# Expert slots without a token gather a row of their own number instead of row 0

## The chip, the core and the metric

The kernel runs on one core of a Trainium2 chip. The metric is the device time of one execution in microseconds; the figure for a kernel is the median of its runs. The profile is one further execution, recorded by the hardware profiler. Clock values are the granted TensorE clock as a share of full speed.

## What is computed

The reference is two transformer layers on 2048 tokens of width 128, all in float32. Layer 0 is attention with 16 heads and then a mixture of 16 experts; layer 1 is causal attention with 8 heads and then a token-shift block. What matters here is the expert part of layer 0, cut to its core:

```python
logits = hidden @ router_w.T                      # 2048 x 16
top_vals, top_idx = top_k(logits, 1)              # one expert a token
scores = sigmoid(logits at top_idx, -inf elsewhere)
routed_in = hidden[None] * scores.T[:, :, None]
gate, up = split(einsum('nth,nhf->ntf', routed_in, gate_up_proj), 2)
routed_out = einsum('ntf,nfh->nth', up * silu(gate), down_proj)
out = shared_ffn(hidden) + routed_out.sum(axis=0)
```

The router's choice for the reference's inputs gives the experts 0 to 15 these numbers of tokens: 101, 145, 126, 158, 178, 94, 189, 85, 135, 99, 88, 198, 96, 132, 123, 101.

## The kernel before

**Slots.** The kernel sorts tokens by expert. It has `SLOTS = 31` slots of 128 rows, which is what 2048 tokens on 16 experts need at worst. Each expert takes as many whole slots as it needs, in the order of the experts. For the counts above that is 23 slots (0 to 22); slots 23 to 30 hold no token, and the last slot of an expert is partly filled (slot 2 holds 17 tokens, slot 13 holds 7, slot 20 holds 4). 31 x 128 = 3968 rows stand for 2048 tokens, so 1920 rows are spare.

**From place to row number.** Lines 850 to 872 work out on DVE the place `slot` of each token, its slot's start `hi` and its row in the slot `lo`. Line 877 compares `hi` with the starts of all slots (`in_tile`, 1 where token and slot belong together), line 881 multiplies this by the token's number (`in_tile_r`), line 887 compares `lo` with 0 to 127 (`at`), and line 890 multiplies the two on PE: 16 matmuls, one per 128 tokens, add up in PSUM tile `tok_ps` (128 x 32). Each entry is the number of the token that stands at this row of this slot. Nothing adds to a spare entry: it stays 0. Line 893 turns the table into whole numbers, `tok`.

**Gather and experts.** Line 912 issues 31 indirect DMAs from POOL, one per slot: each reads 128 rows of 512 bytes from the DRAM tensor `hs_rows` (the scaled tokens, written at line 782) at the numbers in one column of `tok`, into `xs`. Slots go through PE in quads of four: `gathered` (line 926) turns the four tiles (transposes L921, copied out of PSUM by ACT L923) and loads the number of each slot's expert into a PE register (L929); `up_gate` (L935) multiplies by the expert's weights, `silu_up` works on ACT and DVE (L804 to L806), `turn_act` transposes the result (L921, ACT copy L923), `down` (L948) multiplies again, and DVE L952 and an SP DMA (L953) send the rows to `y_rows`. The loop (line 956) takes quads 0 to 7 in order, with `up_gate(q)`, `down(q - 2)`, `gathered(q + 1)`, a step of the shared FFN (L826, L814) at even q, and `turn_act(q - 1)`. At the end 16 more indirect DMAs (L970) fetch each token's row from `y_rows` into `yx`, which DVE adds to `x` (L987). Rows of spare entries are computed and written to `y_rows` too, and never fetched.

**Order.** Each engine works in the order that the framework's scheduler gave its instructions; an instruction that waits holds back what stands behind it on the same engine. The indirect DMAs have POOL's queue to themselves in this stage; the `y_rows` writes have SP's.

Of the kernel before, what the change touches and what calls it, by code (L numbers as in the profile page):

```python
# [9 lines left out]
F32 = mybir.dt.float32  # L10
F32R = mybir.dt.float32r
# [3 lines left out]
ALU = mybir.AluOpType  # L15
# [3 lines left out]
P = 128  # L19
T = 2048  # L20
NT = T // P
# [21 lines left out]
def two_layers(ctx: ExitStack, tc: tile.TileContext, a: dict, out: bass.AP):  # L43
    nc = tc.nc
# [104 lines left out]
    token = const.tile([P, NT], F32, name="token")  # L149
# [594 lines left out]

    hT = h1[:, HOFF:]

    a1 = ctx.enter_context(ExitStack())
# [6 lines left out]
    with ExitStack() as s:  # L756
        rp = s.enter_context(tc.tile_pool(name="route", bufs=1))
# [6 lines left out]
        pt = s.enter_context(tc.tile_pool(name="moet", bufs=2, space=PSUM))  # L764
# [8 lines left out]
        for b in range(NB):  # L773
            ps = pt.tile([P, QB], F32, name=f"hs_ps{b}", tag="t")
            for i in range(TB):
                t = b * TB + i
                nc.tensor.transpose(ps[:, i * P:(i + 1) * P], hT[:, t * P:(t + 1) * P], ident)
            for i in range(TB):
                t = b * TB + i
# [6 lines left out]
        ps = po.tile([P, QB], F32, name="gb_ps", tag="y")  # L786
# [58 lines left out]
        for t in range(NT):  # L845
            nc.tensor.matmul(pos[:, t + 1:, :], ones_r,
                             mine[:, t:t + 1, :].to_broadcast([P, NT - t, NE]),
                             start=False, stop=(t == NT - 1), skip_group_check=True)
# [20 lines left out]
        hi = rp.tile([P, NT], F32, name="hi")  # L869
# [3 lines left out]


        NSL = SLOTS + 1
        in_tile = rp.tile([P, NT, NSL], F32, name="in_tile")
        nc.vector.tensor_tensor(in_tile, hi.unsqueeze(2).to_broadcast([P, NT, NSL]),
                                iota[:, :NSL].unsqueeze(1).to_broadcast([P, NT, NSL]),
                                ALU.is_equal)
        in_tile_r = rp.tile([P, NT, NSL], F32R, name="in_tile_r")  # L880
        nc.vector.tensor_tensor(in_tile_r, in_tile,
                                token.unsqueeze(2).to_broadcast([P, NT, NSL]), ALU.mult)
        at = rp.tile([P, NT, P], F32R, name="at")
        ps = pt.tile([P, NSL], F32, name="tok_ps", tag="t")
        for b in range(NB):
            cols = slice(b * TB, (b + 1) * TB)
            nc.vector.tensor_tensor(at[:, cols, :], lo[:, cols].unsqueeze(2).to_broadcast([P, TB, P]),
                                    units.unsqueeze(1).to_broadcast([P, TB, P]), ALU.is_equal)
        for t in range(NT):
            nc.tensor.matmul(ps, at[:, t, :], in_tile_r[:, t, :], start=(t == 0),  # L890
                             stop=(t == NT - 1))
        tok = rp.tile([P, NSL], U32, name="tok")
        nc.vector.tensor_copy(tok, ps)

        passed = rp.tile([1, SLOTS, NE], F32, name="passed")
        nc.vector.tensor_tensor(passed, iota[:1, :SLOTS].unsqueeze(2).to_broadcast([1, SLOTS, NE]),
# [135 lines left out]
    with ExitStack() as s:  # L1032
        rp = s.enter_context(tc.tile_pool(name="mixc", bufs=1))
# [4 lines left out]
        for b in range(NB):  # L1038
# [3 lines left out]
            for i in range(2):  # L1042
                t = wp.tile([P, QB], F32, name=f"mt{b}{i}", tag=f"mt{i}")
# [16 lines left out]
            t = wp.tile([P, QB], F32, name=f"ft{b}", tag="ft")  # L1060
# [69 lines left out]
```

## Time and profile before

| what | value |
|---|---|
| median of 3 runs | 1290.14 us (1289.53, 1290.14, 1297.87) |
| the profiled execution's own time | 1296.39 us |
| its span, first to last instruction | 1294.7 us |
| mean granted clock | 0.933 |
| PE busy | 1166.7 us, 90% |
| DVE busy | 958.2 us, 74% |
| ACT busy | 776.4 us, 60% |
| POOL busy | 112.3 us, 9% |
| `xs` gathers (L912) | 31 issues, 849.4 to 887.1 us |
| `yx` gathers (L970) | 16 issues, 936.8 to 955.5 us |

The span falls into attention of layer 0 (to about 815 us), the expert stage (about 815 to 960 us), attention of layer 1 and the last block. Start times in the views count from the span's start. In a timeline row the bracket at the end is the idle time of the engine before this row and what ended it; "issue" is time in which the profile shows nothing that the engine waited for, "remote" a semaphore update whose sender the profile could not name. Ends of matmuls are modelled.

### The profile page before, as it was taken

The page shows a single profiled execution, that of the slowest core. Times are in us where ns is not written, and L with a number is a line of the kernel's source. Part 1 is how long each engine was busy: PE and PEld are TensorE (multiplying, and loading weights), DVE is VectorE, ACT ScalarE, POOL GpSimd, SP SyncE. Part 2 cuts the span into 40 slices and gives each one's busy share as a digit, 9 for nine tenths or more (in the row PEclk, how much of TensorE's full clock was granted, in tenths as well). Part 3 has the DMA queues.
Part 4 walks back from the last instruction along what each step waited for, and adds up shares of the span by engine and source line. Part 5 has one row for each costly group of instructions (what it writes and reads, how often), then busy time and mean ns, then how long its engine had stood idle before and what let it go on. Part 6 is the DMA issues. An engine that isn't in the chain of part 4 may idle for free.

```text
span 1294.7 us, 22355 instructions
## 1 busy us (share of the span) xinstructions
PE 1166.7 (90%) x9243; PEld 528.8 (41%) x9243; DVE 958.2 (74%) x1494; ACT 776.4 (60%) x857; POOL 112.3 (9%) x173
## 2 busy tenths in 40 slices
PE   5579999999999999999999999854977999999986
PEld 3233443444334344334434434533643444444432
DVE  4788888989888898898898841531468779897225
ACT  6117777777777777777777787401312355656763
POOL 2010000000000000000000000253041111100113
PEclk9659999999999999999999999876976799999998
DMA  4831000000000010000000000413211001000001
GB/s 127 112 37 34 3 2 2 2 19 18 1 2 2 3 34 2 2 2 2 2 2 1 2 2 1 131 38 34 57 31 33 19 15 29 7 1 1 2 1 32
DMA packets 25317, 27.38 MB, mean 21 GB/s; under 512 B 5328, under 2 KB 18896, under 8 KB 24704
## 3 DMA queue, kind: packets, MB, share of 16 engines
q1 hardware_dynamic: 21440, 20.50, 7.4%
q0 software_dynamic: 1504, 3.08, 1.6%
q10 hardware_dynamic: 2272, 2.36, 0.8%
q8 instruction: 73, 1.20, 0.4%
q14 instruction: 28, 0.23, 0.1%
HBM read 9.88 MB, written 4.13 MB: 11 GB/s over the span
## 4 chain that ended last, share of the span: by engine, by line
PE 77%; DVE 11%; ACT 4%; issue 3%; another core or an unknown queue 2%; DMA 1%; POOL 1%; POOLq 0%; ACTq 0%; DVEq 0%; SPq 0%
PE a0bank L468 23%; PE a0p L442 17%; PE a0p L377 12%; PE a1bank L468 5%; PE a1p L442 4%; DVE a0mx L381 3%; PE a1p L377 2%; DVE a1mx L381 2%; PE a1p L448 2%; DVE a1masked L386 2%; PE sg L826 2%; ACT a0e L452 1%; PE gu L935 1%; PE a0bank L499 1%
## 5 line engine op out<-in xcount | busy, mean ns | idle before, releaser
L381 DVE TENSOR_REDUCE a0mx<-a0p 128x2 f32<-128x1024 f32 x512 | 623.6, 1224 | 78.0 <-PE a0p L377 68.4
L452 ACT ACTIVATE a0e<-a0p 128x1024 f32<-128x1024 f32 x512 | 521.7, 1024 | 172.5 <-PE a0p L442 147.2
L468 PE MATMUL a0bank<-a0e,vA 128*32 128x256 f32 x4096 | 333.6, 392 | 0.6 <-ACT a0e L452 0.6
L377 PE MATMUL a0p<-kS,a0qS 64*128 64x512 f32 x1024 | 248.2, 481 | 26.4 <-DVE a0mx L381 13.4
L442 PE MATMUL a0p<-a0qS,kS 64*128 64x512 f32 x1024 | 259.8, 497 | 0.0
L452 ACT ACTIVATE a1e<-a1p 128x1024 f32<-128x1024 f32 (+3 forms) x160 | 143.1, 896 | 97.4 <-PE a1p L448 94.4
L442 PEld LDWEIGHTS a0p<-a0qS,kS 64*128 64x128 f32 x1024 | 97.1, 184 | 204.3 <-issue 128.8
L377 PEld LDWEIGHTS a0p<-kS,a0qS 64*128 64x128 f32 x1024 | 100.3, 192 | 111.3 <-ACT a0e L452 58.1
L468 PEld LDWEIGHTS a0bank<-a0e,vA 128*32 128x32 f32 x4096 | 86.4, 108 | 139.2 <-issue 124.9
L381 DVE TENSOR_REDUCE a1mx<-a1p 128x2 f32<-128x1024 f32 x96 | 115.6, 1222 | 20.8 <-PE a1p L377 19.9
L468 PE MATMUL a1bank<-a1e,vA 128*32 128x256 f32 (+1 forms) x1152 | 97.5, 385 | 0.5 <-POOL a1e L455 0.4
L442 PE MATMUL a1p<-a1qS,kS 64*128 64x512 f32 (+3 forms) x320 | 76.4, 472 | 3.1 <-DVE a1mx L381 1.9
L377 PE MATMUL a1p<-kS,a1qS 64*128 64x512 f32 (+3 forms) x320 | 68.3, 429 | 7.1 <-DVE a1mx L386 4.1
L386 DVE CUSTOM_DVE_ANT_0 a1masked<-a1p,later 128x128 f32<-128x128 f32 (+3 forms) x128 | 62.5, 489 | 13.3 <-PE a1p L377 8.5
L977 POOL MEMSET vA<- 128x16 f32 x1 | 0.1, 128 | 718.4 <-PE a0bank L520 718.4
L448 PE MATMUL a1p<-a1mT,a1ones 64*128 64x512 f32 (+3 forms) x320 | 61.8, 378 | 0.0
L442 PEld LDWEIGHTS a1p<-a1qS,kS 64*128 64x128 f32 x320 | 31.1, 190 | 60.9 <-issue 33.4
L377 PEld LDWEIGHTS a1p<-kS,a1qS 64*128 64x128 f32 x320 | 32.7, 199 | 36.1 <-DVE a1mx L386 10.3
L455 POOL TENSOR_SCALAR_AFFINE_SELECT a1e<-a1e 128x256 f32<-128x256 f32 x64 | 26.0, 406 | 233.7 <-ACT a1e L452 233.7
L468 PEld LDWEIGHTS a1bank<-a1e,vA 128*32 128x32 f32 x1152 | 25.4, 108 | 43.0 <-issue 32.8
L935 PE MATMUL gu<-wgu_sb,xsT 128*128 x62 | 18.5, 451 | 20.0 <-issue 19.5
L411 ACT CAST a0mT<-a0bank 8x512 fp32r<-8x512 f32 x16 | 9.2, 574 | 45.4 <-PE a0bank L410 45.3
(330 smaller groups left out, 795.7 us busy)
## 6 DMA issues: line engine op xcount, KB each, us to landing
kS<-a0qS SPq DMA_DIRECT2D x28, 128.0 KB
wgu_sb<-in_gate_up SPq DMA_DIRECT2D x1, 2048.0 KB
a0qS<-a0qh SPq DMA_DIRECT2D x62, 32.0 KB
a0qS<-a0ql SPq DMA_DIRECT2D x62, 32.0 KB
y_rows<-y SPq DMA_DIRECT2D x7, 256.0 KB
a1qS<-a1qh SPq DMA_DIRECT2D x24, 64.0 KB
a1qS<-a1ql SPq DMA_DIRECT2D x24, 64.0 KB
hs_rows<-hs SPq DMA_DIRECT2D x4, 256.0 KB
```

The source lines that it names most:

```text
L377: nc.tensor.matmul(ps[:, j, :n], qS[b][r:r + RT, st, i * P:(i + 1) * P], kS(st)[r:r + RT, kb * QB:kb * QB + n], start=True, stop=True)
L381: nc.vector.tensor_reduce(pm[:, i, 2 * pair:2 * pair + 2, kb], ps, AX.X, ALU.max)
L386: nc.vector.tensor_tensor_reduce(masked[:, :n], ps[:, j, :n], later[:, QB - n:], 1.0, LOWEST, ALU.add, ALU.max, pm[:, i, g, kb:kb + 1])
L411: nc.scalar.copy(mT, ps[:nm_rows])
L442: nc.tensor.matmul(ps[:, j, q0:], kS(st)[r:r + RT, kt * P:(kt + 1) * P], qS[b][r:r + RT, st, q0:], start=True, stop=fused)
L448: nc.tensor.matmul(ps[:, j, q0:], ones[r:r + RT, g // S, :], shift[u][r:r + RT, q0:], start=False, stop=True)
L452: nc.scalar.activation(e[:, :, q0:], ps[:, :, q0:], AF.Exp, scale=scale)
L455: nc.gpsimd.affine_select(out=e[:, :, q0:q0 + P], in_=e[:, :, q0:q0 + P], compare_op=ALU.is_ge, fill=0.0, base=0, pattern=[[0, 2], [1, P]] ...
L468: nc.tensor.matmul(av[g * W:(g + 1) * W, c0:c1], vA(kt, grp * HG + g), held[kt, g // 2][:, g % 2, c0:c1], start=(kt == 0 and c0 == 0), sto ...
L499: nc.tensor.transpose(ps[:, i * P:(i + 1) * P], o[:, i * P:(i + 1) * P], ident)
L826: nc.tensor.matmul(ps[:, j, :], w[:, k * P:(k + 1) * P], hT[:, b * QB:(b + 1) * QB], start=True, stop=True)
L935: nc.tensor.matmul(ps[:, i, :], xsT[q][:, i * P:(i + 1) * P], wgu[:, bass.ds(regs[j], 1), :].rearrange("p a f -> p (a f)"), start=True, st ...
```

## The change

The table of row numbers gets a second half. `in_tile` now holds both factors side by side, the comparison (index 1) and its product with the token number (index 0), so one matmul of 64 columns instead of 32 gives the token number and the count of tokens (1 or 0) for each entry. DVE then computes `spare` = (count - 1) x token and subtracts it from the number. For a filled entry `spare` is 0. For a spare entry in row p of slot j the result is `token[p, j mod 16]` = 128 x (j mod 16) + p instead of 0. So the 128 entries of an unused slot read 128 different, adjacent rows of `hs_rows`. The number of DMAs and the bytes that they move stay as they are.

```diff
         NSL = SLOTS + 1
-        in_tile = rp.tile([P, NT, NSL], F32, name="in_tile")
-        nc.vector.tensor_tensor(in_tile, hi.unsqueeze(2).to_broadcast([P, NT, NSL]),
+        in_tile = rp.tile([P, NT, 2, NSL], F32R, name="in_tile")
+        nc.vector.tensor_tensor(in_tile[:, :, 1, :], hi.unsqueeze(2).to_broadcast([P, NT, NSL]),
                                 iota[:, :NSL].unsqueeze(1).to_broadcast([P, NT, NSL]),
                                 ALU.is_equal)
-        in_tile_r = rp.tile([P, NT, NSL], F32R, name="in_tile_r")
-        nc.vector.tensor_tensor(in_tile_r, in_tile,
+        nc.vector.tensor_tensor(in_tile[:, :, 0, :], in_tile[:, :, 1, :].bitcast(F32),
                                 token.unsqueeze(2).to_broadcast([P, NT, NSL]), ALU.mult)
         at = rp.tile([P, NT, P], F32R, name="at")
-        ps = pt.tile([P, NSL], F32, name="tok_ps", tag="t")
+        ps = pt.tile([P, 2, NSL], F32, name="tok_ps", tag="t")
...
-            nc.tensor.matmul(ps, at[:, t, :], in_tile_r[:, t, :], start=(t == 0),
+            nc.tensor.matmul(ps, at[:, t, :], in_tile[:, t, :, :], start=(t == 0),
                              stop=(t == NT - 1))
+        spare = rp.tile([P, NSL], F32, name="spare")
+        nc.vector.scalar_tensor_tensor(
+            spare.rearrange("p (c t) -> p c t", t=NT),
+            ps[:, 1, :].rearrange("p (c t) -> p c t", t=NT), 1.0,
+            token.unsqueeze(1).to_broadcast([P, NSL // NT, NT]), ALU.subtract, ALU.mult)
+        nc.vector.tensor_tensor(spare, ps[:, 0, :], spare, ALU.subtract)
         tok = rp.tile([P, NSL], U32, name="tok")
-        nc.vector.tensor_copy(tok, ps)
+        nc.vector.tensor_copy(tok, spare)
```

The scheduler's order moves a little with it. On DVE one step of the shared FFN (`sigs`, L805) now stands before the first new instruction and its partner (`acts`, L806) between the first and the second; before, both stood behind `tok`. On PE two of the register loads of L929 move from behind quad 3's transposes to the places ahead of and between the transposes of quad 0, and two of the four matmuls of a shared sum (L814) move forward by about 20 instructions.

## The prediction

> **What bounds the kernel now.** I read the windows of the expert stage first, then the chain of waits, the timeline, and last the DMA view, because the change touches only what the 31 gathers read. Over the whole span PE is the bound (90% busy). In the stretch in which the gathers run it is not. The chain of waits in that stretch:
>
> ```profile
> 862.31 1.73 PE sg L826 x4
> 864.09 13.50 another core or an unknown queue
> 877.61 0.60 ACT sige L804
> 878.20 4.28 another core or an unknown queue
> 882.49 2.82 issue
> 885.30 0.58 ACT xsT L923
> 885.89 7.10 another core or an unknown queue
> 893.08 0.58 ACT actT L923
> ```
>
> Columns are start, length, what. From 864.09 to 893.08 the path holds 27.7 us (13.50 + 4.28 + 2.82 + 7.10) that belong to no work of this core. The timeline shows which engine is late:
>
> ```profile
> 865.99 0.49 PE L921 MATMUL xsT_ps<-ident,xs 128*128 128x128 f32 x3
> 866.32 0.60 PE L921 MATMUL actT_ps<-ident,acte 128*128 128x128 f32 x4
> ...
> 877.61 0.60 ACT L804 ACTIVATE sige<-gu 128x512 f32<-128x512 f32 x1 [12.94 <-remote]
> ...
> 885.30 0.58 ACT L923 COPY xsT<-xsT_ps 128x512 f32<-128x512 f32 x1 [7.10 <-issue]
> ...
> 885.94 3.57 PE L935 MATMUL gu<-wgu_sb,xsT 128*128 x8 [19.02 <-issue]
> 887.11 0.95 POOL L912 DMA_INDIRECT xs<-hs_rows,tok  x1 [0.30 <-issue]
> ...
> 893.07 0.58 ACT L923 COPY actT<-actT_ps 128x512 f32<-128x512 f32 x1 [7.18 <-remote]
> ...
> 893.79 2.05 PE L948 MATMUL y_ps<-wdn_sb,actT 128*128 x8 [4.28 <-ACT actT L923]
> ```
>
> PE turned quad 2's tiles at 865.99 to 866.48, but ACT copied them at 885.30; it turned quad 0's `act` by 866.92, but ACT copied it at 893.07. ACT was idle in between. PE's completions reached the others up to 26 us late, and PE stood idle for 19.02 and 4.28 us, in a ring: it waits for ACT, which waits for PE's signal. Nowhere else in the trace does ACT or DVE show a "remote" wait. It ends at 893.1. What else ends there is in the DMA view: first 880 to 893 us (the last gathers), then 937 to 950 us (the `yx` gathers, 16 per-token reads of all different rows), then windows of POOL with its columns busy, PEclk, DMA share, GB/s:
>
> ```profile
> DMA packets 249, 0.52 MB, mean 40 GB/s; under 512 B 121, under 2 KB 121, under 8 KB 249
> q0 software_dynamic: 249, 0.52, 76.7%
> ```
> ```profile
> DMA packets 313, 0.66 MB, mean 51 GB/s; under 512 B 152, under 2 KB 152, under 8 KB 312
> q0 software_dynamic: 312, 0.66, 17.2%
> ```
> ```profile
> 866.00:880.00 14.00, 10.65 (x12) 0.72 0.23 52
> 880.00:893.00 13.00, 6.22 (x7) 0.63 0.77 40
> 937.00:957.00 20.00, 15.00 (x17) 0.83 0.17 50
> ```
>
> The large packets carry 4 KB each (0.52 MB / 128), 16 to a 64 KB gather. In 880 to 893 us one costs 0.767 x 13 us x 16 engines / (249 - 121) = 1.25 us of an engine's time; in 937 to 950 us 0.172 x 13 x 16 / (312 - 152) = 0.22 us. So late gathers take 5 to 6 times as long per byte as other gathers of the same size. POOL issues a gather every 1.25 us (849.44 to 887.11 in 30 steps), slots 23 to 30, which hold no token, from 849.44 + 23 x 1.256 = 878.3 us on; with about 2 us to the first packet that is just where the share jumps. All 128 reads of such a slot go to the same 512 bytes. The gathers then need their whole spacing, queue up, and the last ends at 893, 5.9 us after its issue; slot 3, issued at 853.41, was transposed at 856.24, 2.8 us after.
>
> **The change, part by part.**
> - *Longer way to `tok`.* Removed: one cast from PSUM (L893, 0.19 us). Added: one `scalar_tensor_tensor` and one `tensor_tensor` of 128x32 and the cast from SBUF. No row has these two; the cast of the same size (0.19) is the nearest, the 128x4 rows of L215 (0.14) and the 128x512 rows (0.68) are the ends. The order moves `sigs` (0.68) ahead, into DVE's idle 0.47 us before `tok`, and `acts` (0.69) between. From 848.49: `sigs` to 849.1, first new one to 849.3, `acts` to 849.9, second to 850.1, cast to 850.26, against 849.15 before: +1.1 us, bounds +0.7 (the two `acts`/`sigs` overlap as in the trace, small ones at 0.14) and +2.1 (both new ones at 0.68). POOL's first gather waits for `tok`, behind it all 31, so each slot is 1.1 us later.
> - *Matmuls of 64 columns (L890).* 16 x 0.11 us apart at full clock with 32 columns; those of L846, 16 to 256 columns, take 1.72 us for 16, also 0.11 each. Only the last four follow the last DVE piece: 0, at most 4 x 0.11 = 0.4 us.
> - *Wider `in_tile`.* Same elements, halves interleaved: two at 0.68 as before. 0; if stride cost half as much again, 0.7 us.
> - *Two register loads moved (L929).* 0.30 us each in the trace, with the register work behind it at most 0.7. What hides them is PE's wait for the first slots: `tok`'s matmuls end at 848.93, slot 0's transpose starts at 853.21, 1.1 us later after the change, and PE has eight L814 matmuls (2.07 us) to do between: 0; uncovered, 1.4.
> - *The moved sum (two of four L814 matmuls).* Same work in idle PE: 0.
> - *Gathers.* 31 as before, same bytes, no new wait on any queue; SP's `y_rows` writes start later, after quad 0. What goes is the 1.25 against 0.22 us a packet. Directly: the last slot lands 3.4 us (slot 2's: 852.16 to 855.56, itself 111 spare rows) after its issue instead of 5.9, 2.5 us earlier. That is not on the path while PE's completions are late. Indirectly: the late completions, where the trace has no row for the cause. End one: none of the 23.3 us idle of PE goes. Other end: all of it goes. In between: what lies after 880, where packets are slow, goes, and the stop of 866 to 877.6, when shares were still 0.23, stays. I take this middle: the tail ends with the slow packets to 0.1 us, but the stall's beginning precedes the empty slots by 14 us. Then ACT's copy follows `sige` at 878.2 instead of 885.30 (7.1 us), and `actT` and the 4.28 us wait go with it: 11.4 us. Slot 15 (issued 868.39) is long there, so the next late thing is PE itself, whose order then runs with 0 to 1 us waits to quad 7 (slot 30 at about 891.6, needed later). After that everything follows: `y_rows`, the `yx` gathers behind the last write (936.79), the DVE adds.
> - *Sum.* -11.4 + 1.1 = -10.3 us. On the profiled execution (1296.39, span 1294.7 and 1.7 around it) that is 1286.1. It stands 6.25 above the median of 1290.14, and the runs lie 8 us apart (1289.53 to 1297.87) like the steps of the stall (877.61, 885.30, 893.07, 7.7 apart): an estimate that a run's stall differs by a step. From the median, with the same stall in it: 1279.8. If the median run already lacks 6.25 us of the stall that goes: 1286.1 again. I take **1280**: nothing in the trace says which part of the stall a shorter run would lack, and the median is what is measured; the other end stays in the range.
>
> A rule that speaks against: the Trainium skill, DMA: Bandwidth & Descriptors, "Anatomy of one DMA — SWDGE (gpsimd) path", gives a DMA about 2.0 us plus bytes over 436 GB/s, and has no term for which rows are read. By its figures a 64 KB gather is an estimated 2.15 us whatever the addresses, the 1.25 us issue stays the limit, and the sum would be +1.1, or 1291.2. The packets above (1.25 against 0.22 us at one size) contradict that, so the sum goes by them.
>
> **The rivals.**
> - *All of the stall is the hot row's work* (partly filled slots too: slots 2, 13 and 20 have 111, 121 and 124 spare rows). For: "remote" waits exist only here, never in the 16 `yx` gathers at the same pace. Against: it starts before slot 13's data. Then 23.3 us go; next late is quad 3, slot 15 at 868.39 + 2.8 + 1.1 = 872.3 against PE free at about 871.4: 0.9 back, and 1.1 for `tok`: -21.3, so 1268.8 from the median, 1275.1 from the profiled run; 1270.
> - *The other side: the stall is not the rows'*, but comes of gathers as such beside PE (register loads, completions). For: begins at DMA share 0.23, near the 0.17 to 0.20 of `yx`. Then the late signals hold the path whatever the packets take and +1.1 (0.7 to 2.1, with the 0.4) is all: 1291.2, up to 1293. It decides if PE's copies of quad 2 still stand 10 us or more behind its transposes past 880.
> - *Nothing is different*: the spare rows are still one row. The formula gives 128 x (j mod 16) + p, so this is out; that distinct rows read slower than the 0.22 us row is near nothing.
>
> **How the numbers follow.** Chances: middle 0.36 (1276 to 1287), all of it 0.30 (1265 to 1276), no gain 0.27 (1289 to 1293), something longer 0.04, more than all 0.03. A measurement tells about 1% from no change, here 1277.2 and 1303. Faster: 0.30 + 0.03 and 0.06 of the middle = 0.39; slower 0.04; same 0.57. For 8 in 10: 1266 to 1293, leaving the lowest of the full case and the worst of the rest.
>
> **What would show it.** In the changed profile: `tok` cast about 1.1 us later; DMA share flat at 0.17 to 0.25 from the first gather to the last, none at 0.77; last packet about 3 us after the last issue; ACT's copy of quad 2 within a few us of 878 (middle), at 868 (all) or 885 and later (none). I am wrong if packets stay at 1.25 us, or if they fall to 0.22 and the "remote" waits remain.

## The result and the profile after

The changed kernel takes 1298.05 us (median of 20 runs, 1290.35 to 1302.69); the kernel before, run beside it, 1298.34 us (20 runs, 1286.97 to 1302.89). The ratio is 1.0003, 95% interval 0.998 to 1.0025: no difference that can be told. The three runs of before that the prediction had, median 1290.14, lay low among the twenty. The profiled run of after took 1301.97 us (span 1300.3).

What the rows did is as forecast. Windows of POOL over the gathers of after (POOL busy, PEclk, DMA share, GB/s; the last is the `yx` stage):

```profile
853.00:868.00 15.00, 11.32 (x12) 0.64 0.19 52
868.00:883.00 15.00, 11.32 (x12) 0.70 0.20 52
883.00:896.00 13.00, 5.66 (x6) 0.50 0.12 35
939.00:959.00 20.00, 14.46 (x17) 0.83 0.20 54
```

And the DMA view of 883 to 896 us:

```profile
DMA packets 224, 0.46 MB, mean 35 GB/s; under 512 B 112, under 2 KB 112, under 8 KB 224
...
q0 software_dynamic: 224, 0.46, 11.8%
```

The share is flat where before it rose to 0.77. By the prediction's formula a large packet now costs 0.118 x 13 x 16 / 112 = 0.22 us instead of 1.25, the same as in the `yx` gathers, and the last packet of the gathers ends at 891.6 us. But the wait that the slow packets were held to cause is still there. The chain of waits of after:

```profile
866.63 16.92 another core or an unknown queue
...
883.58 0.60 ACT sige L805
884.17 7.11 another core or an unknown queue
...
891.30 0.58 ACT xsT L929
891.89 3.62 another core or an unknown queue
...
895.58 0.59 ACT actT L929
```

16.92 + 7.11 + 3.62 = 27.65 us belong to no work of the core; before it was 27.7. The timeline of after (here and below, `...` stands for rows left out):

```profile
868.22 0.49 PE L927 MATMUL xsT_ps<-ident,xs 128*128 128x128 f32 x3
...
868.54 0.60 PE L927 MATMUL actT_ps<-ident,acte 128*128 128x128 f32 x4
...
883.58 0.60 ACT L805 ACTIVATE sige<-gu 128x512 f32<-128x512 f32 x1 [16.37 <-remote]
...
891.30 0.58 ACT L929 COPY xsT<-xsT_ps 128x512 f32<-128x512 f32 x1 [7.13 <-remote]
...
891.94 3.78 PE L941 MATMUL gu<-wgu_sb,xsT 128*128 x8 [22.28 <-issue]
...
895.58 0.58 ACT L929 COPY actT<-actT_ps 128x512 f32<-128x512 f32 x1 [3.69 <-remote]
...
896.31 2.05 PE L954 MATMUL y_ps<-wdn_sb,actT 128*128 x8 [0.59 <-ACT actT L929]
```

PE is done with quad 2's transposes by 868.7, and ACT copies them at 891.30. PE's idle time is 22.28 + 0.59 = 22.87 us against 19.02 + 4.28 = 23.30 before. Only its split is new. The trace also records the updates of PE's semaphore: none between 866.59 and 883.55 us, then single ones at 883.55, 886.38, 888.49, 891.28 and 895.51, where PE had ended a `gu`, three transposes of quad 2 and the transposes of `act` from 868.38 to 869.14. Such records are not complete, but ACT starts 0.02 to 0.07 us behind the first, the fourth and the fifth: what is late is PE's signal, not ACT.

The longer way to `tok`, in the timeline of before and of after:

```profile
844.20 0.68 DVE L877 TENSOR_TENSOR in_tile<-hi,iota 128x512 f32<-128x512 f32 x1
...
848.96 0.19 DVE L893 CAST tok<-tok_ps 128x32 uint32<-128x32 f32 x1 [0.47 <-PE tok_ps L890]
```
```profile
845.50 0.68 DVE L878 TENSOR_TENSOR in_tile<-hi,iota 128x512 fp32r<-128x512 f32 x1
...
850.31 0.18 DVE L893 SCALAR_TENSOR_TENSOR spare<-tok_ps,token 128x32 f32<-128x32 f32 x1
...
851.03 0.18 DVE L897 TENSOR_TENSOR spare<-tok_ps,spare 128x32 f32<-128x32 f32 x1
851.25 0.18 DVE L899 CAST tok<-spare 128x32 uint32<-128x32 f32 x1
```

From the start of the first `in_tile` to the end of the cast it is 5.93 us; before, 849.15 - 844.20 = 4.95. So the change costs 0.98 us here; in a second profile of after (`r4_after`, fourth group) the same way takes 5.93 us again. The other 1.3 us by which the cast is later had come about ahead of the change's place (`in_tile` at 845.50 against 844.20).

### The profile page after: what moved, and what is told of

Same layout as the page of the kernel before. It is cut to its first block, busy times and chain, and to the rows that moved or that the text cites. A ratio compares the mean times of both kernels' runs of the same rounds, so it can differ in the third digit from the quotient of the medians.

```text
span 1300.3 us, 22357 instructions
## 1 busy us (share of the span) xinstructions
PE 1172.6 (90%) x9243; PEld 531.7 (41%) x9243; DVE 958.1 (74%) x1496; ACT 776.9 (60%) x857; POOL 112.3 (9%) x173
## 4 chain that ended last, share of the span: by engine, by line
PE 78%; DVE 11%; ACT 4%; issue 2%; another core or an unknown queue 2%; POOL 1%; DMA 1%; ACTq 0%; POOLq 0%; SPq 0%; DVEq 0%
PE a0bank L468 23%; PE a0p L442 17%; PE a0p L377 12%; PE a1bank L468 5%; PE a1p L442 4%; DVE a0mx L381 3%; PE a1p L377 3%; DVE a1mx L381 2%; PE a1p L448 2%; PE sg L827 2%; DVE a1masked L386 1%; ACT a0e L452 1%; PE gu L941 1%; PE a0bank L499 1%
```

## The experiments

The question was what makes PE's signals late, since the hot row does not. Theories: **A**, PE's register loads amid the gathers; **B**, POOL's gathers, once some 13 have been issued; **C**, something in PE's own program at that place. Each group of runs was made on one chip, with the kernel before run on it too.

### First group: the gathers taken away, or part of them

Kernel before on this chip: 1296.21 us. Experts as constants:

```
-                regs[j] = nc.tensor.value_load(expert[0:1, j:j + 1], min_val=0, max_val=NE - 1)
+                regs[j] = ([0, 1, 1, 2, 3, 3, 4, ...] + [15] * 9)[j]
-                                 wgu[:, bass.ds(regs[j], 1), :].rearrange("p a f -> p (a f)"),
+                                 wgu[:, regs[j]:regs[j] + 1, :].rearrange("p a f -> p (a f)"),
```

> The changed kernel with the experts of the 31 slots written in as constants (those of these inputs), so that PE reads no register in the expert stage; the gathers stay. Theory A, PE's register loads amid the gathers hold its signals back: ACT's copy of quad 2 stands within 2 us of its transposes, PE's 22.3 us wait is gone, and the time falls by about 22 us from the changed kernel (1298 to about 1276). Theory B, the gathers do it once some 13 of them have been issued, whatever PE reads: the wait stays at 19 to 23 us and the time within 3 us of the changed kernel.

Measured (10 runs): 1287.89 us, ratio 0.9951 (0.9927 to 0.9974). Its timeline:

```profile
863.72 1.96 PE L941 MATMUL gu<-wgu_sb,xsT 128*128 128x256 f32 x8
...
874.70 0.60 ACT L805 ACTIVATE sige<-gu 128x512 f32<-128x512 f32 x1 [10.36 <-remote]
...
880.37 0.59 ACT L929 COPY xsT<-xsT_ps 128x512 f32<-128x512 f32 x1 [5.07 <-remote]
...
881.01 3.78 PE L941 MATMUL gu<-wgu_sb,xsT 128*128 128x256 f32 x8 [13.40 <-issue]
```

PE reads no register in this stage, and its signals are still 9 us and more late: A falls. The time is 8.3 us lower, between the two forecasts. By the traces some 2.8 us of it lie in a shorter stall (ACT's last late copy starts 41.1 us after the first gather, 43.9 in after) and some 5.4 us behind it (37.3 us from there to the first `yx` gather, 42.7 in after).

The 31 gathers replaced by plain loads of SP:

```
-            nc.gpsimd.indirect_dma_start(out=xs[:, j, :], ...)
+            nc.sync.dma_start(out=xs[:, j, :], in_=a["hs_rows"][r:r + P, :])
```

> The changed kernel with the 31 gathers replaced by 31 plain loads of 128 rows each on SP's queue, of rows that do not belong to the slots, so the experts work on the wrong tokens; register loads stay. Theory A (register loads alone are enough, beside any DMA): the late signals stay, 15 us or more. Theory B (POOL's gathers are needed): no remote wait over 2 us in the expert stage, and the time falls by about 22 us or more, since the plain loads also land sooner.

Measured (4 runs): 1264.62 us, ratio 0.978 (0.9737 to 0.9822): 31.6 us less. No wait of ACT is put down to "remote"; its group for `sige` over 845 to 925 us (busy us, mean ns of one, idle time before and what ended it):

```profile
L805 ACT ACTIVATE sige<-gu 128x512 f32<-128x512 f32 (+1 forms) x8 | 4.7, 584 | 14.3 <-PE gu L940 14.3
```

Only slots 0 to 12 gathered (and the other tiles zeroed):

```
-        for j in range(SLOTS):
+        nc.vector.memset(xs[:, 13:, :], 0.0)
+        for j in range(13):
```

> The changed kernel with only the gathers of slots 0 to 12; the tiles of the others are zeroed, so most of the experts' work is on zeros. Theory B (a count: late once a 14th gather is issued): no late signals, time about 22 us less. Theory A (register loads beside gathers under way): the load that follows quad 2's transposes comes at about 868.3, when the 13th gather has just been issued and is still under way: signals late until it has landed, about 2 to 3 us, then on time, so about 19 us less. Theory C (something else in PE's program at that place, gathers not needed): the 22 us wait stays.

Measured (4 runs): 1276.18 us, ratio 0.9868 (0.9827 to 0.991). ACT's groups over the same time:

```profile
...
L805 ACT ACTIVATE sige<-gu 128x512 f32<-128x512 f32 (+1 forms) x8 | 4.7, 584 | 16.0 <-PE gu L942 13.8 <-PE actT_ps L928 2.2
L930 ACT COPY actT<-actT_ps 128x512 f32<-128x512 f32 (+1 forms) x8 | 4.6, 574 | 6.9 <-PE actT_ps L928 6.9
L930 ACT COPY xsT<-xsT_ps 128x512 f32<-128x512 f32 (+1 forms) x8 | 4.6, 571 | 21.6 <-PE xsT_ps L928 21.6
```

Every wait ends with named work of PE, none with "remote", though PE's part of the code is unchanged: C falls, and 20 us go. The same with `range(23)`:

> The changed kernel without the gathers of the 8 slots that hold no token (their tiles are zeroed), so only the order of POOL's work is shorter by 8 gathers of 1.25 us. If the late signals end when the gathers have drained (theories A and B): the wait ends about 10 us earlier, ACT's copies at about 881 instead of 891, time about 10 us less. If it ends by PE's own program: unchanged, 22 us.

Measured: 1286.86 us, ratio 0.9925 (0.99 to 0.995).

```profile
882.44 0.60 ACT L805 ACTIVATE sige<-gu 128x512 f32<-128x512 f32 x1 [16.07 <-remote]
...
883.40 0.60 ACT L930 COPY actT<-actT_ps 128x512 f32<-128x512 f32 x1
```

Counted from the first gather, ACT's last late copy comes after 33.5 us (883.40 - 849.89) instead of 43.9 in after (895.58 - 851.72): 10.4 us sooner, with 8 gathers of 1.25 us fewer. The lateness starts in the same place and lasts as long as POOL issues gathers, and 4 to 5 us more (from the end of the last issue to the last late signal 3.9 us here, 5.2 in after).

### Second group: the gathers spread or emptied

Kernel before: 1296.02 us. Two kernels were to break the train, and did not:

```
+            if j in (12, 24):
+                nc.gpsimd.tensor_copy(seen, xs[:, j - 1, :1])
```

> The changed kernel with POOL's train of 31 gathers cut into three: before slots 12 and 24 POOL copies one column of the slot before, and so waits until that gather has landed (about 2.5 us after its issue). If what holds PE's signals is a count of gathers with no gap between them (14 in the changed kernel): no remote wait over 2 us, PE's 22.3 us wait gone, 1298 to about 1277 (two pauses of 1.5 us are hidden, since quad 3's slots come long before PE needs them). If it is a count since the start of the stage, whatever has landed: late signals again from the 14th gather on, time 1296 to 1302.

```profile
870.11 0.20 POOL L920 COPY seen<-xs 128x1 f32<-128x1 f32 x1
...
885.18 0.20 POOL L920 COPY seen<-xs 128x1 f32<-128x1 f32 x1
```

The scheduler put the copies behind gathers 16 and 28 (issued at 869.18 and 884.24), where the data had long landed, so POOL waited for nothing. PE's late signals had begun at 867.6. Measured: 1295.06 us, 0.9991 (0.9964 to 1.0017). Inconclusive on a pause; 0.2 us of other work behind the 16th gather doesn't end the lateness. The same edit in the kernel before:

> The kernel before (token 0's row in every spare place) with the same two pauses. It says what the change would be worth where PE's signals are on time. If the hot row costs by itself: its last gathers land up to 6 us after their issue, and the time is 1 to 5 us above the paused changed kernel. If it costs nothing: within 1 to 2 us of it, or 1 us below for the shorter way to tok. With the late signals gone both stand near 1277.

Measured: 1294.53 us, 0.9996 (0.9967 to 1.0024). It tells as little, for the same reason.

```
+            nc.gpsimd.memset(idle, 0.0)
```

> The changed kernel with a 128x512 memset on POOL ahead of every gather, so that a gather is issued about every 1.8 to 2.2 us instead of every 1.25. If a count without a gap matters whatever the pace: signals late from the 14th gather, which now stands at about 851.7 + 13 x 2.0 = 878 us. If the rate matters (more than one gather under way at a time): no late signals at all and about 20 us less, as far as the last slots are not late for PE. If it is PE's own program: late at 868 us as before.

Measured: 1298.6 us, 1.0015 (0.9989 to 1.0041). POOL did the memsets ahead of the first gather, and the gathers kept their 1.25 us. Nothing was tested.

Spare places left out by a bound, so that their reads don't take place:

```
+        nc.gpsimd.memset(xs, 0.0)
+        far = rp.tile([P, NT], F32, name="far")
+        nc.gpsimd.memset(far, 4096.0)
-            token.unsqueeze(1).to_broadcast([P, NSL // NT, NT]), ALU.subtract, ALU.mult)
+            far.unsqueeze(1).to_broadcast([P, NSL // NT, NT]), ALU.subtract, ALU.mult)
...
-                in_offset=bass.IndirectOffsetOnAxis(ap=tok[:, j:j + 1], axis=0))
+                in_offset=bass.IndirectOffsetOnAxis(ap=tok[:, j:j + 1], axis=0),
+                bounds_check=T - 1, oob_is_err=False)
```

> The changed kernel, but spare places get row number 4096, above a bound, so that the gather leaves them out, and xs is zeroed on POOL ahead of time; 31 gather instructions, 2048 rows instead of 3968. If what counts are the rows: the last 8 gathers move nothing, the late signals end about 10 us earlier, time about 10 us less than the changed kernel. If what counts is the instructions on POOL: late until the 31st, 1296 to 1300. The bound's own work may lengthen an issue beyond 1.25 us.

Measured: 1294.25 us, 0.9977 (0.9949 to 1.0006); a gather is issued every 1.30 us.

```profile
882.86 0.58 ACT L933 COPY xsT<-xsT_ps 128x512 f32<-128x512 f32 x1 [5.03 <-remote]
...
892.04 0.59 ACT L933 COPY actT<-actT_ps 128x512 f32<-128x512 f32 x1 [8.60 <-remote]
...
897.67 0.60 ACT L805 ACTIVATE sige<-gu 128x512 f32<-128x512 f32 x1 [5.04 <-remote]
```

From slot 23 on (issued from 883.68) no row is moved (the DMA view has 0.00 MB from 885.5 to 898 us), and the signals are late up to 897.6 all the same. So neither the rows nor the bytes keep them late; the gather instructions on POOL are enough for that. Whether a train that moves no row at all would start it was not run.

### Third group: a train with gaps that can't be moved

Now the row numbers of the later slots are made from what an earlier gather wrote, so the order is a data dependence:

```
+            if j in (12, 24):
+                n = min(12, SLOTS - j)
+                tokg = rp.tile([P, n], U32, name="tokg")
+                gate = rp.tile([P, n], F32, name="gate")
+                nc.gpsimd.tensor_scalar(gate, xs[:, j - 1, :n], 0.0, None, ALU.mult)
+                nc.gpsimd.tensor_tensor(gate, gate, spare[:, j:j + n], ALU.add)
+                nc.gpsimd.tensor_copy(tokg, gate)
+            i_ap = tok[:, j:j + 1] if j < 12 else tokg[:, j % 12:j % 12 + 1]
```

> The changed kernel, with row numbers of slots 12 to 23 made on POOL from a column that gather 11 wrote, and those of 24 to 30 from one that gather 23 wrote: three small POOL operations that can't move ahead, so POOL stands still twice, some 2.5 us each, until all is landed. If the count of gathers without a gap decides: no signal later than 2 us, PE's long wait gone, 1298 to about 1280. If the gathers' number since the start of the stage decides, or PE's own place in its program: late signals from the second quad's gu on as before, ending some 5 to 6 us later, 1300 to 1306.

Second kernel: the same three operations ahead of every quad from 2 on, reading `xsT[q - 2]` in place of `xs`, and that quad's gathers behind them:

> The changed kernel with the gathers of quad q (from 2 on) held until ACT has copied quad q - 2 turned: bursts of 4 gathers with gaps. If gathers without a gap are what holds PE's signals: on time throughout, and about 15 to 20 us less, unless slots come late for PE (each quad needs 5 us of issue and 2.5 us of landing, in 11 to 13 us). If the number alone decides: late from about the 14th gather, which PE reaches later, and 1300 to 1310.

Third kernel: 8 gathers of known rows into a tile of their own, ahead of `in_tile`:

```
+        for j in range(8):
+            nc.gpsimd.indirect_dma_start(
+                out=extra[:, j, :], out_offset=None, in_=a["hs_rows"],
+                in_offset=bass.IndirectOffsetOnAxis(ap=own[:, j:j + 1], axis=0))
```

> The changed kernel with 8 more gathers, of rows known ahead into a tile that nobody reads, in POOL's idle time ahead of the row numbers (they land before slot 0's is issued, if POOL is as idle there as before). If the number of gathers since the start decides: the signals are late from the 6th real gather on, at about 858 us, in quad 0 already. If the gathers without a gap or PE's place in its program decide: late from quad 1's gu at about 868 as before.

Measured: 1271.95, 1272.86 and 1269.63 us (one run). But the kernel before took 1269.47 us on this chip (19 runs, 1261.75 to 1272.34), 27 us less than on the others. The timeline of the third kernel, whose train is uncut:

```profile
865.34 1.96 PE L948 MATMUL gu<-wgu_sb,xsT 128*128 x8
...
867.34 0.60 ACT L805 ACTIVATE sige<-gu 128x512 f32<-128x512 f32 x1 [1.54 <-PE gu L948]
...
867.97 0.59 ACT L936 COPY xsT<-xsT_ps 128x512 f32<-128x512 f32 x1
...
868.46 0.59 ACT L936 COPY actT<-actT_ps 128x512 f32<-128x512 f32 x1
...
868.84 1.89 PE L948 MATMUL gu<-wgu_sb,xsT 128*128 x8
```

The copies follow PE within a microsecond although gathers come every 1.25 us up to 888.7. On this chip PE's signals are not late at all, so the group could not tell why they are elsewhere. Between the medians the gaps cost 2.5 and 3.4 us here: ratio 1.002 (1.0 to 1.0039) and 1.002 (0.9996 to 1.0045), which both reach down to no difference.

### Fourth group: the same where signals are late

> The changed kernel again, beside the kernel before on the same chip. If this chip holds PE's signals back, both stand near 1296 to 1300, ratio 1.000, as recorded. If not, both stand near 1270: the longer way to the row numbers then costs its 1.1 us in full (ratio 1.001), unless the hot row's slow last gathers were late for PE there, in which case the change gains those 1 to 5 us (ratio 0.996 to 1.000).

> As x3_gateq (quad q's gathers held until quad q - 2 has been copied). On a chip with late signals: if gathers without a gap hold them, on time and 1270 to 1280; if the number of gathers alone decides, 1297 or more. On a chip without: 1273, 3 us over the kernel before, as measured.

> As x3_gate (POOL stands still until all is landed ahead of slots 12 and 24). On a chip with late signals: if a count without a gap decides, on time and about 1272 to 1280; if the number since the start or PE's place decides, 1297 to 1306. On a chip without: 1272.

> As x3_pre8 (8 more gathers ahead, landed early). On a chip with late signals: if the number since the start decides, late from the 6th real gather (about 858 us) and longer than the changed kernel by up to 8 us; if not, late from quad 1's gu at about 868 as before, within 2 us of the changed kernel. On a chip without: 1269 to 1271.

This chip holds them back: in the changed kernel ACT copies quad 2 at 888.73 us, 20.3 us behind PE's transposes. The kernel before takes 1295.91 us. Measured (the two kernels with gaps in 4 runs each): after 1294.96, ratio 0.9992 (0.9975 to 1.0009); gaps by quads 1271.89, 0.9826 (0.98 to 0.9852); two gaps 1272.45 (one of the four at 1283.17), 0.9846 (0.9808 to 0.9883); 8 gathers ahead 1297.17, 0.9996 (0.9978 to 1.0014). The kernel with two gaps, where the `gate` line is POOL standing until gather 11 has landed:

```profile
866.16 1.89 PE L949 MATMUL gu<-wgu_sb,xsT 128*128 x8
...
867.15 0.25 POOL L922 TENSOR_SCALAR gate<-xs 128x12 f32<-128x12 f32 x1 [1.71 <-DMA xs<-hs_rows,tok]
...
868.09 0.60 ACT L805 ACTIVATE sige<-gu 128x512 f32<-128x512 f32 x1 [1.24 <-PE gu L949]
...
868.58 0.58 ACT L937 COPY xsT<-xsT_ps 128x512 f32<-128x512 f32 x1
...
869.04 0.60 ACT L937 COPY actT<-actT_ps 128x512 f32<-128x512 f32 x1
...
869.21 1.99 PE L949 MATMUL gu<-wgu_sb,xsT 128*128 x8
```

The kernel with 8 gathers ahead, uncut:

```profile
868.09 1.89 PE L948 MATMUL gu<-wgu_sb,xsT 128*128 x8
...
870.14 0.60 PE L934 MATMUL actT_ps<-ident,acte 128*128 128x128 f32 x4
...
887.28 0.60 ACT L805 ACTIVATE sige<-gu 128x512 f32<-128x512 f32 x1 [18.50 <-remote]
...
894.28 0.59 ACT L936 COPY xsT<-xsT_ps 128x512 f32<-128x512 f32 x1 [6.40 <-remote]
...
894.92 3.78 PE L948 MATMUL gu<-wgu_sb,xsT 128*128 x8 [23.73 <-ACT xsT L936]
```

All 31 gathers take place in both. With a stop after 12 the signals are on time and 23 us are gone, nearly all that the chips differ by. With 8 more ahead, landed before the train began, the lateness begins where it did. So the cause, on the chips that show it, is a train of gathers without a gap; the number since the start of the stage is not. What counts in the gap, POOL's rest, the landing of all gathers or the three small operations, is not told apart here.

### Fifth group: the change where nothing is late

> The changed kernel with the two pauses of r4_gate, again, for the comparison with the next two on one chip: 1270 to 1273, signals on time.

> The kernel before with the same two pauses (its row numbers kept in a second copy, one more cast of 128x32 on DVE, behind the one that releases the gathers), so token 0's row is read in every spare place. Signals on time, about 1270 to 1272. If the change is worth something there (theory: the hot row's slow packets are late for PE in the last quad): 1 to 4 us above r5_gate, with PE's wait for quad 7's slots in the trace. If it costs only its longer way to tok: 1 us below r5_gate, last gather landing 5 us or more after its issue, but PE not waiting for it.

> As r5_gate, but the three small POOL operations ahead of slots 12 and 24 read a column that the gather four before wrote, which has landed, so POOL works on something else for about 0.9 us instead of standing 2.5 us with all landed. If the gathers must have landed: late signals again, about 1296 on a chip that has them. If any break in the train is enough: on time, and 0 to 2 us below r5_gate.

The second kernel is the one before with the same gates; the third reads `xs[:, j - 4, :n]` in place of `xs[:, j - 1, :n]`. The chip was one without late signals: the kernel before 1269.60 us. Measured: 1273.76, ratio 1.0032 (1.0012 to 1.0052); with the hot row 1277.20, 1.0066 (1.0043 to 1.009); short gaps 1270.61, 1.0003 (0.9982 to 1.0023). The view of the tile `xs` from 876 to 906 us, its line on how long gathers took to land, of the first kernel and of the one with the hot row:

```profile
DMA to landing us min/median/max: 2.4/2.5/4.2
```
```profile
DMA to landing us min/median/max: 2.5/5.5/8.2
```

And the timeline of the one with the hot row, then of the first, at the last quad that waited:

```profile
897.05 0.33 PE L931 MATMUL xsT_ps<-ident,xs 128*128 128x128 f32 x1 [1.74 <-DMA xs<-hs_rows,tokg]
```
```profile
894.33 0.33 PE L935 MATMUL xsT_ps<-ident,xs 128*128 128x128 f32 x1 [0.55 <-DMA xs<-hs_rows,tokg]
```

Here the hot row is late for PE, and the change is worth 3.4 us between the medians (12 and 7 runs; the intervals overlap by 0.0009). The profiled run of the kernel with the hot row, 1268.91 us, is its shortest, yet from the first `xs` gather to the first `yx` gather it takes 70.4 us, the first kernel 64.7. That is with both pauses, which push the last gathers back and of which the second waits for a hot gather. Whether the short gaps cure the late signals stays open: this chip has none. On such a chip the change without gaps ran only as part of the third group's kernel with 8 gathers ahead, and once: 1269.63 us against 1269.47.

## Why the prediction was wrong

- **The step that failed is "Indirectly: the late completions".** It let the late end of the stall go with the slow packets (-11.4 us) because both ended within 0.1 us. That term measured 0: after has the fast packets and 27.65 us without named work, against 27.7. Its last packet ends at 891.6 us and the stall 3.9 us later, at 895.5. Before, the two met by coincidence, each some 5 us behind the end of POOL's last issue: the packets because they were slow, the stall as in after (5.2 us). The stall's end goes with the end of POOL's train: with 23 gathers in place of 31 the stall ends 10.4 us sooner, and with rows left out it stays. The rival *The other side* was right, and its test came out as written: ACT's copy of quad 2 stands 22.6 us behind PE's transposes. Its evidence, a stall that begins at a DMA share of 0.23, should have weighed more than the coincidence of ends.
- **The count against it was misread.** "Never in the 16 `yx` gathers at the same pace" was taken to speak for the hot row. A train of 13 showed nothing either, and the late signals set in at the 13th to 15th gather (the first late one is always that of quad 1's `gu`: done at 868.4 in after, 14 gathers issued; at 865.7 with constant experts, 13 issued; at 867.7 with 23 gathers, 15 issued). So a train of 16 leaves next to no time for them. That is inferred; no train of between 13 and 23 gathers was run.
- **The base was 8 us low.** The sum was made from a median of three runs, 1290.14; twenty gave 1298.34. The rival that came true, +1.1, would have been 1299.4 from there, 1.4 above the measured 1298.05. From the three runs it was 1291.2, so the range's upper end of 1293 missed even though that case was in it. The estimate that a run's stall differs by a step, which was to explain the spread, isn't borne out: where no signal is late the runs lie as far apart as those three (the kernel before in the fifth group 1261.55 to 1271.63), and on both kinds of chip short runs have a higher granted clock (after 1290.35 us at 0.938, 1302.17 at 0.924; the kernel before in the fifth group 1261.55 at 0.951, 1271.63 at 0.941).
- **Right:** `tok` +1.1 us (measured 0.98, in two profiles; the two new operations 0.18 us each); the wider `in_tile` 0 (0.68 us as before); the matmuls of 64 columns 0 (`tok_ps` is done 4.46 us after the start of `in_tile`, 4.73 before); the packets, 0.22 us instead of 1.25, share flat; the moved loads and sums 0. The 0.98 us is not seen in the end time, in which runs of one kernel lie 12 to 16 us apart.
- **The price of the full stall** was put at 22.4 us (23.3 less 0.9). The chips differ by 26.5 us (1296.0 against 1269.5 for the kernel before), near the 27.7 us that the chain of waits named; on one chip, two gaps take 22.5 us off the changed kernel (1294.96 to 1272.45).
- **The rule weighed:** the Trainium skill, DMA: Bandwidth & Descriptors, "Anatomy of one DMA — SWDGE (gpsimd) path", gives an estimated 2.15 us for such a gather whatever its addresses. Distinct rows agree within 0.4 us (median 2.5 us in the fifth group); 128 reads of one row do not (5.5). Its sum, no gain, was nearer the truth, but not because the addresses don't count: they do, off the path.

Open: what in POOL's work delays PE's signals, and why chips differ. Each of the five chips was measured in one group only, so that the time of measuring and not the chip makes the difference is not excluded. No view shows the cause; "remote" is only the profile's word for a releaser that it cannot name.

## What to carry to other kernels

A wait whose releaser the profile can't name should be priced by taking its suspected cause away in thought at both its ends: a cause that begins after the wait does can't be the whole of it, and two things that end together may share a third. A train of POOL gathers is best cut by a real data dependence, as operations without one are moved by the scheduler: against the kernel before, the changed kernel with two gaps was 1.5% faster where signals were late (0.9846) and 0.2 to 0.3% slower where they were not (1.002, 1.0032). Before a base is fixed from few runs, their spread is to be put into the range, and a chip-dependent wait calls for a second chip.

## What the runs showed of the hardware

- On three of the five chips of these groups, PE's signals to ACT and DVE came up to some 26 us late while POOL issued gathers without a gap every 1.25 us, from the 13th to 15th on and until 2 to 5 us after the last issue; signals of ACT to PE did not (in after ACT's copy ends at 891.89, PE starts at 891.94). On two chips they were on time with the same train. The kernel before takes 1296 us on the one kind and 1269.5 on the other.
- 128 reads of one 512-byte row cost a 4 KB packet 1.25 us of a DMA engine against 0.22 us for different rows, and gathers took 5.5 us to land instead of 2.5 (medians of the fifth group).
- A gather whose rows are all left out by its bound still takes POOL 1.30 us to issue.
- Constant experts in place of 31 register loads on PE are worth 8.3 us here, some 2.8 of them by a shorter stall.
